# 160 small TensorE products without a reader, ahead of the first product and behind the last one

## The chip, the core and the metric

The kernel runs on one core of one Trainium2 chip. A core has five engines that work side by side, each with its own list of instructions in a fixed order: TensorE (PE, with its weight loads shown as PEld), VectorE (DVE), ScalarE (ACT), GpSimd (POOL) and SyncE (SP), which here only issues transfers. They wait for each other by semaphores. The metric is the time of one execution on the device in microseconds (us), and of a kernel the median of its runs.

## What is computed

The input is x of 16 batches with 512 tokens of 512 features in fp32. Each token is normalized and conditioned in six ways, by tables of gains and biases that two indices and a mask pick per token, and by three small networks on per-batch vectors. The six results are weighted, joined, and pass a two-layer network with silu and a last normalization; x is added. Cut to its core:

```python
h = _ln(x, pw_g[pathway_ids], pw_b[pathway_ids])
h = _ln(h, cp_g[compartment_ids], cp_b[compartment_ids])
t = _ln(x, tm_g[time_steps], tm_b[time_steps])
m = x + _mlp_ln(memory_state, ...)[:, None, :]       # and n, r alike
s = _ln(x, ms_g[scale_type], ms_b[scale_type])
w = jax.nn.softmax(aw)
cat = jnp.concatenate([w[0]*h, w[1]*t, w[2]*m, w[3]*n, w[4]*r, w[5]*s], axis=-1)
return x + _mlp_ln(cat, int_W1, int_b1, int_W2, int_b2, int_g, int_be)
```

`_ln` subtracts the mean, divides by the root of the variance plus 1e-5, and applies gain and bias. `_mlp_ln` is `silu(s @ W1 + b1) @ W2 + b2`, normalized.

## The kernel before

The 8192 tokens are sorted by their combination of two indices (15 groups, `NG`), so that a tile of 128 sorted tokens shares its tables nearly everywhere. The sorted tokens are worked on in 16 windows (`NW`) of four tiles each. For every window rows of x and of the tables are gathered by indirect DMA from POOL's queue, DVE and ACT normalize, DVE turns 32 by 32 blocks, SP's queue spreads the turned blocks over the partitions (L205), and TensorE multiplies: first layer in L404 and L452, second layer in L546, and for the last tiles L487. POOL scatters the finished rows to their places (L638). Which step stands behind which is written out by hand in three lists of names (ORDER, WINDOW, LAST); every engine works off its part of that order.

Ahead of the windows stands a start of some 70 us. The places of the tokens are counted there:

- POOL writes constants: `iota` tables, and `ident`, a 128 by 128 identity, written twice (`make_identity`, once among the constant tiles and once more in L727).
- DVE compares every token's group with all 15 groups (L798) and scans the result (L807).
- TensorE's first two products, L810 and L811, add up the counts of the partitions in front (`pc`); L815 and L816 add up the groups' beginnings (`pbg`).
- DVE adds `pc` to the scan (L829), masks it (L830) and reduces it to each token's place (L832).
- L845 is the first layer of the three small networks (`ph`). L896 multiplies one-hot tables, eight at a time, which DVE builds in L883 to L887; their sum `pn` is the sorted list of tokens, which everything behind it needs (the gathers of x among it).

At the end, the last window's second layer runs on TensorE in L487, tile by tile. Behind each tile come `last_add` (L607, DVE), the sum of squares (L612, ACT), root and inverse (L588, L596), `end_sum` (L603, DVE) and `put_out` (L638, POOL), which scatters 128 rows. The program ends when the last scatter has landed and the engines have met.

Results of TensorE lie in PSUM, in a pool of eight buffers (`ps`, all with the tag "p") that are handed out in turn: a new tile takes the buffer of the tile eight requests earlier and waits until that one is finished with. `psum(name)` asks for one buffer of 128 by 512. The names that the change touches are `psum`, `ident`, `L` (32, a quarter of the 128 partitions, `P`), and the places behind L809 and behind the last call of `run`.

Two products without a reader are already in the kernel: L1063 and L1069 multiply blocks of `wt` into a tile named `idle`.

Of the kernel before, what the change touches and what calls it, by code (L numbers as in the profile page):

```python
# [81 lines left out]
def kernel(ctx: ExitStack, tc: tile.TileContext, a: dict, out: bass.AP):  # L82
# [24 lines left out]
    nc = tc.nc  # L107
# [6 lines left out]
    L = P // Q  # L114
# [42 lines left out]
    ident = const.tile([P, P], F32, name="ident")  # L157
# [506 lines left out]
    def scratch(k, *shape):  # L664

        n = 1
        for m in shape:
            n *= m
        room, at = rooms[k]
        t = room[:, at : at + n]  # L670
        rooms[k][1] = at + n
        names = "abc"[: len(shape)]
        return t if len(shape) == 1 else t.rearrange(f"p ({' '.join(names)}) -> p {' '.join(names)}",
                                                     **dict(zip(names, shape)))
# [14 lines left out]
    for nm in ("mem", "noi", "res"):  # L689
        k = a[nm + "T"].shape[0]  # L690
        kk = min(k, P)
        n = k // kk
        t = prep.tile([kk, n, B], F32, name="stT" + nm)
        nc.scalar.dma_start(t, a[nm + "T"].rearrange("(c p) b -> p c b", p=kk))
        stT.append(t)
        t = w2[:kk, at : at + n, :]
# [16 lines left out]
    def iota(t, pattern, base=0, step=0):  # L713
        nc.gpsimd.iota(t, pattern, base=base, channel_multiplier=step, allow_small_or_imprecise_dtypes=True)
        return t

    i_row = iota(prep.tile([P, 1], F32, name="i_row"), [[0, 1]], step=1)
    i_col = iota(scratch(1, P), [[1, P]])
    i_grp = prep.tile([P, NG], F32, name="i_grp")
# [87 lines left out]
    nc.vector.tensor_tensor_scan(f_run, f_of, f_of, 0.0, ALU.add, ALU.max)  # L807
    upto = run[:, :, NQ - 1]
    pc = ps.tile([P, NG], F32, tag="p", name="pc")  # L809
    nc.tensor.matmul(pc, below, upto, start=True, stop=False)  # L810
    nc.tensor.matmul(pc[:, 1:], above, upto[:, : NG - 1], start=False, stop=True)  # L811
    nc.scalar.copy(up[:, 1:], upto)
# [639 lines left out]
    def piece(name):  # L1452
        kind, *at = name.split(".")
        if kind in pieces:
            pieces[kind](*map(int, at))
        elif kind in for_window:
            for_window[kind](of(at[0]))
        elif kind in for_tile:
            for_tile[kind](of(at[0]), *map(int, at[1:]))
        elif kind == "wu":  # L1460
            awake(at[0], [int(v) for v in at[1:-1]], int(at[-1]))
        elif kind == "tv":
            turn_v(of(at[0]), int(at[1]), home(at[0], "V"))
        elif kind[0] == "s":
            spread_row(of(at[0]), "r" + kind[1], "c" + kind[1], home(at[0], kind[1]), int(at[1]))
        else:
            layer1(of(at[0]), kind[1], int(at[1]))
# [6 lines left out]
    def run(names, w=None):  # L1474
        for name in names.split():
            kind, *at = name.split(".")
            if w is not None and at and at[0] in FROM:
                v = w + FROM[at[0]]
                if not 0 <= v < NW:
                    continue  # L1480
                name = ".".join([kind, str(v), *at[1:]])
            if name not in done:
                done.add(name)
                piece(name)
# [8 lines left out]
    for w in range(NW - 1):  # L1493
        run(WINDOW, w)
    run(LAST, NW - 1)


# [51 lines left out]
```

## Time and profile before

| what | value |
| --- | --- |
| median of 3 runs | 923.31 us |
| lowest and highest run | 919.57, 925.25 us |
| profiled execution, first to last instruction (its span) | 920.3 us |
| mean granted TensorE clock over the span | 0.994 |
| data moved over the span | 185.40 MB |

Nothing but its span is known of the profiled execution's own time; the span lies 3.0 us under the median and inside the range of the runs. In the profile, PE is TensorE, L followed by a number is a line of the kernel, and times are counted from the first instruction. A row names engine, line, operation, tiles (output, arrow, inputs), the shape on the array for TensorE (rows by columns of the weights), the shape of the moving data and its type. Times in order of time are start and length in us. Instructions of a kind that stand close together are merged into one row with their count; the length is then from the first start to the last end. An fp32 product is two pairs of a weight load and a product on the array, so four products in the code are eight rows on TensorE and eight weight loads.

### The profile page before, as it was taken

The numbers are of one execution on the slowest core, as the hardware profiler recorded it, in microseconds if no ns is written. First come the engines' busy times: TensorE is split into PE (matmuls) and PEld (weight loads), VectorE is DVE, ScalarE is ACT, GpSimd is POOL, SyncE is SP. The second block draws the span as 40 slices with busy tenths as digits, with TensorE's granted clock in tenths as the row PEclk, the third lists the DMA queues.
The fourth block names the chain that finished last, engine by engine and source line by source line (L and its number), as shares of the span: only waits on it lengthen the run. The fifth ranks groups of instructions, "written<-read, shape, count | busy, mean of one in ns | idle before, by whom it ended". The sixth has DMA issues, their size and how long they took to land.

```text
span 920.3 us, 13563 instructions
## 1 busy us (share of the span) xinstructions
PE 884.8 (96%) x3617; PEld 642.0 (70%) x3617; DVE 733.6 (80%) x1360; ACT 521.2 (57%) x1263; POOL 666.9 (72%) x730
## 2 busy tenths in 40 slices
PE   6979899999999999999999999999999999999996
PEld 6634446868677777868686877777686867778682
DVE  8776767878789798978787887869697888879565
ACT  5568736464555738374646556473657566572413
POOL 9876678576768678686878686877767676876452
PEclk9999999999999999999999999999999999999999
DMA  8755677777767777777777777777667776776513
GB/s 272 249 185 179 220 226 197 207 210 204 235 178 232 202 218 195 215 208 202 227 202 227 187 235 191 226 193 216 186 197 210 203 220 191 221 200 190 154 37 113
DMA packets 88557, 185.40 MB, mean 201 GB/s; under 512 B 24324, under 2 KB 24388, under 8 KB 88476
## 3 DMA queue, kind: packets, MB, share of 16 engines
q0 software_dynamic: 31104, 104.88, 39.4%
q1 hardware_dynamic: 56668, 79.53, 29.6%
q8 instruction: 30, 0.49, 0.2%
q14 instruction: 51, 0.42, 0.2%
q10 hardware_dynamic: 704, 0.08, 0.1%
HBM read 100.48 MB, written 19.97 MB: 131 GB/s over the span
## 4 chain that ended last, share of the span: by engine, by line
PE 50%; POOL 5%; DVE 4%; issue 3%; DMA 3%; SPq 2%; ACT 1%; POOLq 0%; DVEq 0%; ACTq 0%
PE u L452 13%; PE p L404 13%; PE p L452 11%; PE pq_0b L546 4%; PE pq_1b L546 4%; PE pq_1a L546 3%; PE pq_0a L546 2%; SPq L205 2%; DMA catZ<-rZ 2%; POOL xbs L391 1%; POOL out L638 1%; DMA pw<-in_pw,i_pw 1%; DVE vs L265 1%; DVE yb L634 0%; DVE yb L633 0%
## 5 line engine op out<-in xcount | busy, mean ns | idle before, releaser
L404 PE MATMUL p<-vs,catV 128*128 128x512 f32 x512 | 228.3, 593 | 3.9 <-DVE vs L265 1.7
L404 PEld LDWEIGHTS p<-vs,catV 128*128 128x128 f32 x512 | 96.9, 190 | 108.5 <-issue 99.6
L452 PE MATMUL p<-wh__81,catH 128*128 128x256 f32 x480 | 111.0, 379 | 0.0
L452 PEld LDWEIGHTS p<-wh__81,catH 128*128 128x128 f32 x480 | 91.4, 190 | 12.2
L376 ACT ACTIVATE pw<-pw,rsh 128x512 f32<-128x512 f32 x64 | 45.6, 714 | 95.2 <-DVE pw L383 76.9
L638 POOL DMA_INDIRECT out<-yb,tok x64 | 75.4, 1178 | 31.2 <-issue 15.1
L475 ACT ACTIVATE add<-add 128x512 f32<-128x512 f32 x64 | 39.7, 625 | 94.4 <-DVE add L472 93.1
L350 ACT ACTIVATE junk<-pw 128x512 bf16<-128x512 f32 x60 | 37.5, 626 | 85.8 <-DVE pw L347 78.1
L171 POOL DMA_INDIRECT cp<-cp_rows,i_cp x64 | 73.4, 1147 | 15.5 <-issue 13.2
L391 POOL TENSOR_TENSOR xbs<-xbs,rows 128x512 f32<-128x512 f32 x64 | 82.4, 1289 | 1.4
L171 POOL DMA_INDIRECT pw<-in_pw,i_pw x64 | 63.0, 984 | 28.1 <-DVE rH L197 13.0
L625 POOL TENSOR_TENSOR rsy<-vey,mhalf 128x4 f32<-128x4 f32 (+1 forms) x16 | 23.6, 1473 | 82.3 <-DVE veh L368 69.5
L171 POOL DMA_INDIRECT xbs<-in_x,tok x64 | 65.1, 1017 | 19.9 <-issue 18.1
L171 POOL DMA_INDIRECT add<-rows,i_add x64 | 67.0, 1048 | 16.6 <-issue 16.5
L383 DVE SCALAR_TENSOR_TENSOR pw<-pw,sumsh,cp 128x512 f32<-128x512 f32 x60 | 45.5, 760 | 32.9 <-DMA cp<-cp_rows,i_cp 32.8
L317 ACT ACTIVATE xm<-xbs,nmx,rsx 128x512 f32<-128x512 f32 x64 | 48.8, 806 | 22.9 <-DVE nmx L311 17.2
L372 POOL TENSOR_TENSOR rsh<-veh,mhalf 128x1 f32<-128x1 f32 x64 | 48.6, 760 | 13.0 <-DVE veh L368 11.5
L347 DVE SCALAR_TENSOR_TENSOR pw<-pw,rsx 128x512 f32<-128x512 f32 x64 | 56.0, 876 | 2.3
L452 PE MATMUL p<-wt,catH 128*128 128x256 f32 x240 | 56.7, 379 | 0.0
L452 PE MATMUL u<-wt,catX 128*128 128x256 f32 x240 | 56.5, 379 | 0.0
L452 PEld LDWEIGHTS u<-wx__80,catX 128*128 128x128 f32 x240 | 45.7, 190 | 12.6 <-issue 3.8
L452 PE MATMUL u<-wt,ss 128*128 128x256 f32 x240 | 54.4, 379 | 0.0
(439 smaller groups left out, 2127.7 us busy)
## 6 DMA issues: line engine op xcount, KB each, us to landing
catX<-rX SPq DMA_DIRECT2D x240, 64.0 KB
catV<-rV SPq DMA_DIRECT2D x240, 64.0 KB
catZ<-rZ SPq DMA_DIRECT2D x240, 64.0 KB
catH<-rH SPq DMA_DIRECT2D x240, 64.0 KB
rows<-adde SPq DMA_DIRECT2D x8, 256.0 KB
yb<-in_int_W SPq DMA_DIRECT2D x1, 1024.0 KB
catH<-in_int_W SPq DMA_DIRECT2D x1, 1024.0 KB
w1x<-in_int_W SPq DMA_DIRECT2D x1, 1024.0 KB
```

What stands on the lines that cost most here:

```text
L171: nc.gpsimd.indirect_dma_start(dst, None, table, bass.IndirectOffsetOnAxis(ap=idx, axis=0), **kw)
L317: nc.scalar.activation(t, st["xb"][:, j, :], AF.Identity, bias=st["nm"][:, j : j + 1], scale=st["rs"][:, j : j + 1])
L347: nc.vector.scalar_tensor_tensor(h, h, st["rs"][:, j : j + 1], pw[:, D:], ALU.mult, ALU.add)
L372: nc.gpsimd.tensor_tensor(rs, st.pop(("ve", j)), mhalf[:, :1], ALU.pow)
L376: nc.scalar.mul(pw[:, :D], pw[:, :D], st.pop(("rs", j)))
L383: nc.vector.scalar_tensor_tensor(pw[:, :D], pw[:, :D], st["sh", j][:, 1], cp, ALU.add, ALU.mult)
L391: nc.gpsimd.tensor_add(st["xb"][:, j, :], st["xb"][:, j, :], rows[:, 2, :])
L404: nc.tensor.matmul(st["p1", g], st["c" + blk][:, g, c, :], m[:, c, :], start=(blk == first and c == order[0]), stop=(blk == last and c == ...
L452: nc.tensor.matmul(dst, m[:, c], at_["half1"][k][:, c], start=(k == 1 and c == 0), stop=(c == NC - 1), skip_group_check=True)
L475: nc.scalar.activation(st["add", g], st["add", g], AF.Silu)
L546: nc.tensor.matmul(st["pq", 2 * p + i][:, half], st["zp", p][k][:, c], at_["half"][k][:, c], start=False, stop=(c == 1), skip_group_check= ...
L638: nc.gpsimd.indirect_dma_start(out_rows[j], bass.IndirectOffsetOnAxis(ap=tok[:, j, w : w + 1], axis=0), yb[:, j, :], None)
```

## The change

A helper asks for a PSUM tile and multiplies a 32 by 32 corner of `ident` with a 32 by 16 corner of it into the tile's first 32 partitions, `n` times into the same place. Nothing reads the result. It is called with 64 ahead of the first product, and with 96 behind the last step.

```diff
+    def idle_products(name, n):
+        t = psum(name)
+        for _ in range(n):
+            nc.tensor.matmul(t[:L, :L // 2], ident[:L, :L], ident[:L, : L // 2], start=True, stop=True)
...
     pc = ps.tile([P, NG], F32, tag="p", name="pc")
+    idle_products("idle0", 64)
     nc.tensor.matmul(pc, below, upto, start=True, stop=False)
...
     run(LAST, NW - 1)
+    idle_products("idle1", 96)
```

What stands on TensorE at the start, before. In brackets are the semaphores that a row waits for, named by the engine or the DMA queue that raises them. `pc`, `pbg` and `ph` are the tiles named above, `up` a column of counts, `room` scratch space, `w` a weight:

```order
L1545 UNCONDITIONAL_BRANCH [waits barrier_Pool_Activation_PE_DVE_SP_release]
L810 MATMUL pc<-vs_86,room_118 128x15 [waits DVE_49]
L811 MATMUL pc<-vs_86,room_118 128x14
L815 MATMUL pbg<-room_118,up 14x1 [waits Activation_49,Pool_49]
L815 MATMUL pbg<-room_118,up 14x1 x2
L816 MATMUL pbg<-up,room_118 128x14
```

And now:

```order
L1552 UNCONDITIONAL_BRANCH [waits barrier_Pool_Activation_PE_DVE_SP_release]
L720 MATMUL idle_232<-ident 32x16 [waits Pool_49]
L720 MATMUL idle_232<-ident 32x16 x63
L816 MATMUL pc<-vs_86,room_118 128x15 [waits DVE_49]
L817 MATMUL pc<-vs_86,room_118 128x14
L821 MATMUL pbg<-room_118,up 14x1 [waits Activation_49,Pool_49]
```

The 64 products wait for POOL once, for `ident`, and stand ahead of `pc` in TensorE's order; the lines behind are numbered 5 or 6 higher. On TensorE at the end, before (`p_15_1` and `p_15_3` are second-layer tiles of the last window, `catV` holds its turned input):

```order
L487 MATMUL p_15_1_8029<-w_82,catV 128x512 x3
L487 MATMUL p_15_3_8034<-w_82,catV 128x512 [waits DMAHW4_49,DMAHW5_49,DMAHW3_49,DMAHW2_49]
L487 MATMUL p_15_3_8034<-w_82,catV 128x512 x3
L1545 UNCONDITIONAL_BRANCH
```

And now:

```order
L487 MATMUL p_15_1_8094<-w_82,catV 128x512 x3
L487 MATMUL p_15_3_8099<-w_82,catV 128x512 [waits DMAHW4_49,DMAHW5_49,DMAHW3_49,DMAHW2_49]
L487 MATMUL p_15_3_8099<-w_82,catV 128x512 x3
L720 MATMUL idle_8136<-ident 32x16 [waits PE_49]
L720 MATMUL idle_8136<-ident 32x16 x95
```

The 96 products stand between the last product and the branch to the end; their first one waits for an earlier TensorE write into the same buffer. Of the instructions that were there before, one got a new wait: the first product of `ptp` (L1014, now L1020) waits for an earlier TensorE write. The other engines' instructions, their order and their waits are as before.

## Prediction

> **What bounds the kernel now.** I read the page first, then the order of time of the first 12 us and of the end, then windows for the clock, and last the TensorE rows whose shapes are near the added one.
>
> The page's first and second part, and the queue that brings instructions:
>
> ```profile
> span 920.3 us, 13563 instructions
> ...
> PE 884.8 (96%) x3617; PEld 642.0 (70%) x3617; DVE 733.6 (80%) x1360; ACT 521.2 (57%) x1263; POOL 666.9 (72%) x730
> ...
> PE   6979899999999999999999999999999999999996
> ...
> PEclk9999999999999999999999999999999999999999
> ...
> q8 instruction: 30, 0.49, 0.2%
> ```
>
> TensorE is busy in all but the first and the last slices, so a shift of the whole program costs its full length, and a delay inside the middle would too. The added work lies in the only two places where TensorE idles for long: ahead of its first product and behind its last. The question is how long these two holes are, and how long 64 and 96 products take in them.
>
> The first 12 us in order of time (start, length, engine, line, operation, and in brackets the idle time and who ended it):
>
> ```profile
> 2.59 0.29 POOL masks.py:199 TENSOR_SCALAR_AFFINE_SELECT ident<-ident 128x128 f32<-128x128 f32 x1
> ...
> 4.97 2.17 DVE L807 TENSOR_TENSOR_SCAN vs<-vs 128x960 f32<-128x960 f32 x1
> ...
> 7.20 0.61 PE L810 MATMUL pc<-vs,room 128*128 128x15 f32 x2 [7.20 <-DVE sm L818]
> ...
> 7.64 0.58 PE L811 MATMUL pc<-vs,room 128*128 128x14 f32 x2
> ...
> 8.27 1.16 DVE L829 TENSOR_TENSOR vs<-vs,pc 128x960 f32<-128x960 f32 x1 [0.49 <-PE pc L811]
> ...
> 9.15 0.32 PE L815 MATMUL pbg<-room,up 128*14 128x1 f32 x6 [0.92 <-POOL tokf L752]
> ...
> 9.46 1.16 DVE L830 TENSOR_TENSOR vs<-vs 128x960 f32<-128x960 f32 x1
> ```
>
> The added products read only ident, whose second writing on POOL ends at 2.59 + 0.29 = 2.88. TensorE's first product, L810, started at 7.20, when DVE's scan L807 was through. So the hole at the start runs from about 2.93 to 7.20, 4.27 us. Who waits behind it is in the same rows: DVE L829 stood idle for 0.49 us until pc was there. Whatever L810 is late, L829 is late.
>
> Windows (busy time of each engine with the number of instructions, then granted clock, DMA share, GB/s):
>
> ```profile
> core 0: us, PE busy (x) PEld busy (x) DVE busy (x) ACT busy (x) POOL busy (x), PEclk, DMA share, GB/s
> ...
> 9.46:31.26 21.80, 21.25 (x147) 20.42 (x146) 21.20 (x35) 15.68 (x47) 20.77 (x41) 1.00 1.04 377
> ...
> 39.50:42.90 3.40, 3.40 (x48) 2.02 (x49) 3.05 (x14) 0.00 (x0) 2.72 (x7) 0.50 0.71 198
> ...
> 56.60:59.90 3.30, 3.30 (x25) 0.92 (x17) 2.17 (x7) 3.30 (x7) 1.97 (x3) 0.50 0.09 24
> ...
> 911.50:916.70 5.20, 0.00 (x0) 0.00 (x0) 3.58 (x7) 1.02 (x3) 2.86 (x3) 1.00 0.26 101
> 916.80:918.50 1.70, 0.00 (x0) 0.00 (x0) 0.00 (x0) 0.00 (x0) 0.00 (x0) 0.50 0.40 154
> 918.50:920.30 1.80, 0.00 (x0) 0.00 (x0) 0.00 (x0) 0.00 (x0) 0.00 (x0) 0.50 0.00 0
> ```
>
> From L829's successor to the end of the one-hot tables DVE is busy 21.20 of 21.80 us: it has no slack to win back a late start. The end of the program, in order of time:
>
> ```profile
> 897.46 13.97 PE L487 MATMUL p<-w,catV 128*128 128x512 f32 x32
> ...
> 914.40 0.82 DVE L603 SCALAR_TENSOR_TENSOR yb<-yg,sd,xbs 128x512 f32<-128x512 f32 x1
> ...
> 915.76 0.96 POOL L638 DMA_INDIRECT out<-yb,tok  x1 [0.30 <-issue]
> ```
>
> The last product ends at 897.46 + 13.97 = 911.43; then come DVE, the last scatter on POOL to 916.72, its landing (a share of 0.40 up to 918.5, none behind it), and 1.8 us of closing steps without work. I let TensorE run until 918.0, in the middle of what is left of the landing, before anything waits for it: the second hole is 6.6 us.
>
> **The change, part by part.** 160 fp32 products make 640 instructions, so each is two weight loads and two products on the array; that is how the page counts its 3617 pairs. For 64 products that is 128 pairs, for 96 it is 192. What does a pair cost? The TensorE rows in order of time:
>
> ```profile
> 9.85 3.58 PE L845 MATMUL ph<-stTmem,w 128*128 128x16 f32 x16
> ...
> 15.56 5.39 PE L896 MATMUL pn<-vs 128*64 128x128 f32 x32 [0.32 <-DVE bi L917]
> ...
> 34.23 0.88 PE L1068 MATMUL pf<-ident,catZ 64*32 64x16 f32 x32
> ...
> 36.68 0.38 PE L1028 MATMUL pgc<-rows,catZ 14*128 14x64 f32 x2
> 36.91 0.38 PE L1029 MATMUL pgc<-rows,room 14*128 14x64 f32 x2
> 37.13 0.38 PE L1028 MATMUL pgc<-rows 14*128 14x64 f32 x2
> ...
> 39.31 1.23 PE L1058 MATMUL pa<-at_n,ident 128*32 128x16 f32 x32 [0.34 <-ACT at_n L1039]
> ```
>
> And two rows of the same load, 128 columns of fp32 weights, grouped by line and shape (the last number ahead of the second bar is the mean ns of one):
>
> ```profile
> L845 PEld LDWEIGHTS ph<-stTmem,w 128*128 128x128 f32 x16 | 3.5, 333 | 0.0
> ...
> L1063 PEld LDWEIGHTS idle<-wt 128*128 128x128 f32 x2 | 0.3, 188 | 0.0
> ```
>
> The load takes 333 ns at 10 us and 188 ns at 33 us. The start runs at a slow clock, although the clock's column stands at 1.00 there. Line L896 alone shows where it ends (its products in flight in each us):
>
> ```profile
> 18.00:19.00 1.00, 1.00 (x6) 1.00 1.05 387
> ...
> 20.00:21.00 1.00, 1.00 (x11) 1.00 1.06 389
> ```
>
> Up to 19 us six are in flight in a microsecond, afterwards eleven. So the first added products meet the slow clock, the last ones a fast one.
>
> The price of a pair at the slow clock: L845's 16 pairs take 3.58 us; less the 0.37 us of the last one that is 3.21 / 15 = 214 ns for weights of 128 columns and only 16 columns of data, so the load sets the pace. The added pair has 32 columns of weights: 214 / 4 = 53.5 ns. At the fast clock the four pairs from the first L1028 to the second take (37.13 - 36.68) / 4 = 112 ns each for 128 columns, so 28 ns for 32. From below both are bounded by rows with 32 columns of weights: L1068, (0.88 - 0.18) / 31 = 23 ns fast, and L1058, (1.23 - 0.21) / 31 = 33 ns in a stretch that is mostly slow (0.50 from 39.5). But these two write to the four quarters of the output in turn, while the added products all use the first 32 rows and the first quarter, one place on the array, as L845 and L1028 use the one whole array. So I take 53.5 slow and 28 fast, and keep 33 and 23 as lower ends.
>
> *Ahead of the first product.* 128 x 53.5 ns = 6.85 us from 2.93 to 9.78. L810 then starts 2.58 us late, L829 as well, and DVE carries it to 31.26. The sum: +2.58. L815, L816 and the ph products stand behind in TensorE's order; pbg had waited 0.92 us for POOL, so it is later by less, and ph has to be through before pn, which DVE's own delay puts at 15.56 + 2.58. Lower end: 128 x 33 = 4.2 us, through at 7.15, nothing late. Below nothing: the slow clock might end sooner; on DVE's path that could shorten only pc's own 1.0 us (8.27 - 7.20), by up to half, so -0.5.
>
> *Behind the last product.* 192 x 28 = 5.4 us, from 911.3 to 916.8, inside the hole of 6.6 us: nothing. What hides it is the last normalization and the scatter with its landing. If that cover is gone, or the clock is slow all the way, 192 x 53.5 = 10.3 us, 3.6 over the hole: +3.6 is the upper end. The clock fell to 0.50 just behind 916.7 here, 5.3 us after the last product, so a slow remainder would be a few products.
>
> *The rest.* The new tile ahead takes one of the eight PSUM buffers in turn; so ptp, the ninth tile instead of the eighth, waits for an earlier TensorE write that has long ended, and the tile behind takes a buffer that its reader left long before. Both cost under 0.1 us. Nothing is changed in the other queues. The 640 instructions need 2.5 more fetches (7234 instructions in 30 packets are 241 each); a fetch's time is 0.002 x 16 x 920 / 30 = 1.0 us of one engine, against 3.6 us in which 128 fast pairs use one up: hidden.
>
> Sum against the profiled execution: 920.3 + 2.6 = 922.9 for the span. The median of the runs, 923.31, stands 3.0 above that span; with the same distance I get 925.9.
>
> **A rule that would make it cheaper.** The row is L845's 214 ns for 128 columns at the slow clock, 112 in L1028. The Trainium skill, "TensorE: Matmul & The Clock Gate", section "LDWEIGHTS (loading the stationary operand)", gives the load as columns divided by 1.2, in ns, whatever the clock: 107 for 128 columns, 27 for 32. By that, an estimate, the first 128 pairs take 3.4 us, end at 6.4 and cost nothing. The fast rows agree with it, the slow ones do not, and the slow ones are at the place in question.
>
> **The rivals.**
>
> *Cheap products.* If the pace is that of L1058 and L1068, 23 to 33 ns, both holes swallow everything: 923.3. For it: the same size of weights. Against it: their four quarters.
>
> *The clock rises under the new products.* The windows show steps that last about 3.4 us (39.5 to 42.9, 56.6 to 59.9). If 3.4 us of unbroken products raise the clock, it is fast from somewhere between 6.3 and 9.8 us. At 8.0, 95 of the 128 pairs are through, the other 33 take 0.9 us: L810 at 8.9, 1.7 late, less some 0.4 in pc: 924.6. Against it: L845 and its successors ran unbroken from 9.85 to beyond 15 us and six a microsecond of L896 still stand at 18 to 19. The same page's section "The HAM clock gate (the "warmup" mystery)" has the rule of about 3.4 us of sustained activity; L845 disagrees if being occupied is enough for it.
>
> *The half-clock steps move.* The steps at 39.5 and 56.6 cost at most half of 3.4 us each; a start that is later by 2.6 us may lose them or win others, 3.4 us either way: 922.5 to 929.3.
>
> *Slower by over 1%.* The place is the first hole, and the mechanism is that products on one PSUM tile wait for each other: each then costs its full duration, 211 ns as in L1058: 128 x 0.211 - 4.27 = +22.7, and 192 x 0.18 - 6.6 = +28 behind the end, 974. With one price p for both, 320 p - 10.9 exceeds 9.2 us from 63 ns on. Against it: L845's products last 374 ns and start every 214, and the two halves of each of them write the same cells.
>
> **How the numbers follow.** Forecast 0.55 (925.9), cheap products 0.18 (923.3), the clock rises 0.10 (924.6), moved steps 0.07, a tail that sticks out 0.05 (929.5), over 1% slower 0.04, and 0.01 for a gain over 1% that none of these explains. About 1% (9.2 us) is what a measurement of this kernel can tell from no change, as its own runs lie 5.7 us apart. The bounds: -0.5 and -3.4 give 919.4, +2.6 and +3.6 give 929.5; I take 920.0 to 930.0, which also holds the runs' own spread around the middle cases. Faster by over 1% would need 9.2 us, more than all the gains named together: 0.01. Within 1%: 0.95. Slower: 0.04.
>
> **What would show it.** Right: the added products run from 2.9 to about 9.8 us at 53 ns, L810 starts 2.6 us later and L829 behind it, pn ends 2.6 us later; at the end the products run from 911.3 plus the shift for 5.4 us, and the closing steps keep their distance from the last scatter. Wrong: L810 at 7.2 as before (cheap), L845's load under 200 ns (clock risen), or a shift at 33 us that is gone by 100 us, since I assume that nothing between holds slack.

## The result, and the profile after

The changed kernel took 925.21 us in the median of 17 runs (921.69 to 928.67), the kernel before 919.85 in as many on the same chip (917.16 to 925.25). The ratio is 1.0051, interval 1.0034 to 1.0067, so the change costs 4.7 us (3.1 to 6.2): within 1%, but not nothing. (A difference in us is here and below the ratio less one, times the median before; the ratio is estimated from the single runs, and is not quite the quotient of the two medians.) The profiled execution took 928.67 us, the longest of the 17.

Its page, first and second part and the queue that brings instructions:

```profile
span 926.8 us, 14203 instructions
...
PE 902.8 (97%) x3937; PEld 658.4 (71%) x3937; DVE 729.8 (79%) x1360; ACT 520.7 (56%) x1263; POOL 667.3 (72%) x730
...
PE   8989999999999999999999999999999999989998
...
q8 instruction: 33, 0.54, 0.3%
```

TensorE has 320 pairs more (3937 against 3617), three fetches more on q8, and the span is 6.5 us longer. The first and the last slice of TensorE are fuller now, as they must be, and that is no gain: the products there are read by nobody.

The start in order of time, DVE's rows first and then TensorE's; L816 was L810 before, L835 was L829, L902 was L896:

```profile
4.97 2.17 DVE L812 TENSOR_TENSOR_SCAN vs<-vs 128x960 f32<-128x960 f32 x1
...
10.94 1.16 DVE L835 TENSOR_TENSOR vs<-vs,pc 128x960 f32<-128x960 f32 x1 [3.16 <-PE pc L817]
```

```profile
2.94 7.01 PE L720 MATMUL idle<-ident 32*32 32x16 f32 x128 [2.94 <-POOL ident masks.py:199]
9.87 0.61 PE L816 MATMUL pc<-vs,room 128*128 128x15 f32 x2
10.32 0.58 PE L817 MATMUL pc<-vs,room 128*128 128x14 f32 x2
...
18.37 6.09 PE L902 MATMUL pn<-vs 128*64 128x128 f32 x32 [1.46 <-DVE bi L923]
```

The scan L812 ends at 7.14 as before, and L816 could start; it starts at 9.87, behind the 128 pairs. DVE's L835 now stands idle for 3.16 us where L829 stood for 0.49: 2.67 more, the same as L816's delay (9.87 against 7.20). That is how a wait is read: the bracket names the tile and the line, and the difference of two such brackets is the price. At L902 it is 2.81 (18.37 against 15.56).

The end in order of time, and the windows over it:

```profile
916.43 7.31 PE L720 MATMUL idle<-ident 32*32 32x16 f32 x192
...
921.36 0.96 POOL L638 DMA_INDIRECT out<-yb,tok  x1 [0.30 <-issue]
```

```profile
916.50:920.90 4.40, 4.40 (x142) 4.40 (x142) 3.54 (x7) 1.02 (x3) 2.29 (x2) 1.00 0.18 63
921.10:923.70 2.60, 2.60 (x50) 2.54 (x48) 0.00 (x0) 0.00 (x0) 0.96 (x1) 0.50 0.54 203
```

Behind the last product the clock falls, 4.5 us later, while small products run: 142 pairs in 4.40 us, then about 50 in 2.60. They end at 923.74. The span ends 926.8 - 921.36 = 5.44 us behind the start of the last scatter; before it was 920.3 - 915.76 = 4.54. So 0.9 us of the loss sits behind that scatter, where I had put nothing. (Spans are given to 0.1 us, so such a distance is good to 0.05 us.)

Was it the products that were waited for, or the landing? The transfers in the 4.0 us from the start of the last scatter (each digit is 0.1 us, the mean busy share of the 16 DMA engines in tenths), the kernel before:

```profile
DMA  0078969972000009799796000000000000000000
...
DMA packets 160, 0.52 MB, mean 131 GB/s; under 512 B 32, under 2 KB 32, under 8 KB 160
```

And the changed kernel:

```profile
DMA  0078979972006009699694400010101000000000
...
DMA packets 161, 0.54 MB, mean 135 GB/s; under 512 B 32, under 2 KB 32, under 8 KB 160
...
q8 instruction: 1, 0.02, 1.5%
```

Each view holds two scatters: 128 rows of 512 fp32 numbers are 0.26 MB, half of the 0.52 MB. The burst up to 1.0 us belongs to the scatter before, whose POOL instruction ran just ahead, and the one from 1.5 us on to the last scatter. (A scatter that stands alone, at 911.66 in the kernel before, moves 80 packets, 0.26 MB, in one burst from 1.5 us on.) Before, it is all through at 2.2 us. In the changed kernel one packet of q8, a fetch of instructions of 0.54 MB / 33 = 16 KB, falls in at 1.2 us, and the last burst trails off up to 3.1 us with digits of 1: nearly all engines are done, a few small pieces are not. (That these are the pieces of the engine that carried the fetch is read from the digits; the view names no engines.) This is 0.9 us, the whole of the difference in distance. The products themselves had ended at 923.74, before 921.36 + 3.1 = 924.46.

That leaves 6.5 - 2.7 - 0.9 = 2.9 us of this execution. The path there was not a constant shift. L1069 (L1063 before), a product without a reader that was there already and stands behind `pn`, starts at 36.19 (33.38 before: +2.81) and the first window's ptH at 107.42 (104.99: +2.43), but near 795 us the shift was gone. The kernel before at these places, in order of time:

```profile
33.38 0.91 PE L1063 MATMUL idle<-wt 128*128 128x384 f32 x2
...
104.99 0.63 PE L1212 MATMUL ptH<-ident,pw 128*128 128x128 f32 x4 [0.86 <-ACTq L320]
...
795.18 7.03 PE L404 MATMUL p<-vs,catV 128*128 128x512 f32 x16
...
828.81 3.62 PE L452 MATMUL u<-wx__80,ss 128*128 128x256 f32 x16
832.26 3.62 PE L452 MATMUL u<-wt,ss 128*128 128x256 f32 x16
```

The changed kernel:

```profile
36.19 0.91 PE L1069 MATMUL idle<-wt 128*128 128x384 f32 x2
...
107.42 0.63 PE L1218 MATMUL ptH<-ident,pw 128*128 128x128 f32 x4 [0.86 <-ACTq L320]
...
794.51 7.03 PE L404 MATMUL p<-vs,catV 128*128 128x512 f32 x16
...
832.12 5.41 PE L452 MATMUL u<-wx__80,ss 128*128 128x256 f32 x16 [3.07 <-DVE ss L433]
837.36 3.62 PE L452 MATMUL u<-wt,ss 128*128 128x256 f32 x16
```

At 795 it is 0.7 us ahead; then TensorE waits 3.07 us for `ss`, and the next 16 products take 5.41 us instead of 3.62. From 0.7 ahead it goes to 837.36 - 832.26 = 5.10 behind. What held `ss` is a load of a window's input (line, awaited transfer, then total, times and longest in us over the whole execution; the longest is the wait here):

```profile
DVE ss L433 <- DMA catV<-rV: 6.9, 3, 5.1
```

Whether a late load there belongs to the change or to this execution is what the first thing to try, the same kernel once more, has to tell.

### The profile page after: what moved, and what is told of

It is laid out like the page before. It is cut to its first block, busy times and chain, and to the rows that moved or that the text cites. A ratio compares the mean times of both kernels' runs of the same rounds, so it can differ in the third digit from the quotient of the medians.

```text
span 926.8 us, 14203 instructions
## 1 busy us (share of the span) xinstructions
PE 902.8 (97%) x3937; PEld 658.4 (71%) x3937; DVE 729.8 (79%) x1360; ACT 520.7 (56%) x1263; POOL 667.3 (72%) x730
## 5 line engine op out<-in xcount | busy, mean ns | idle before, releaser
L452 PE MATMUL u<-wx__80,ss 128*128 128x256 f32 x240 | 56.2, 388 | 3.1 <-DVE ss L433 3.1
```

The source lines that it names most:

```text
L452: nc.tensor.matmul(dst, m[:, c], at_["half1"][k][:, c], start=(k == 1 and c == 0), stop=(c == NC - 1), skip_group_check=True)
```

## The experiments

The theory: the loss is the first hole (128 pairs of 53 ns end 2.7 us after the scan) plus a fetch in the last scatter; the tail's own products cost nothing. Rivals: the products behind the last one stick out; the clock is what the products change; the middle loses (the stall near 830). All kernels are edits of the changed kernel, and each ratio is to the kernel before in runs on the same chip.

| label | products ahead, behind | median (runs), before (runs) | ratio (interval) | in us |
| --- | --- | --- | --- | --- |
| front64 | 64, 0 | 925.46 (12), 923.64 (29) | 1.0021 (1.0001 to 1.0041) | +1.9 (0.1 to 3.8) |
| tail96 | 0, 96 | 921.49 (12), 923.64 (29) | 0.9987 (0.9967 to 1.0007) | -1.2 (-3.0 to 0.6) |
| front32 | 32, 0 | 922.22 (12), 923.64 (29) | 0.9996 (0.9974 to 1.0019) | -0.4 (-2.4 to 1.8) |
| tail192 | 0, 192 | 931.55 (6), 923.64 (29) | 1.0083 (1.0061 to 1.0105) | +7.7 (5.6 to 9.7) |
| again | 64, 96 | 925.40 (12), 921.35 (29) | 1.0036 (1.0014 to 1.0058) | +3.3 (1.3 to 5.3) |
| front128 | 128, 0 | 930.29 (6), 921.35 (29) | 1.0105 (1.0062 to 1.0148) | +9.7 (5.7 to 13.6) |
| wide16 | 16 full-width, 0 | 922.17 (12), 921.35 (29) | 1.0006 (0.9982 to 1.0030) | +0.6 (-1.7 to 2.8) |
| both_fit | 32, 64 | 920.85 (12), 921.35 (29) | 1.0000 (0.9976 to 1.0025) | 0.0 (-2.2 to 2.3) |
| fit64 | 64, 64 | 924.82 (12), 923.56 (17, one of 1899.38 us left out of the ratio) | 1.0032 (1.0000 to 1.0064) | +3.0 (0.0 to 5.9) |

**front64: the products ahead alone.**

```diff
-    idle_products("idle1", 96)
```

> Only the 64 products ahead of the first product; the 96 behind are gone. Theory (the start is late by what the products overrun their hole, 2.7 us, and that is carried to the end): pc starts at 9.87 instead of 7.20, pn ends 2.8 us later, and the time is 2 to 3 us over before. Rival A (the windows take the shift back, and the loss of the changed kernel comes from behind the end): pc is as late, but the time is within 1 us of before. Rival B (the later start moves the half-clock steps and costs more by that): 4 to 5 us over before with more half-clock time than before.

Measured: +1.9 us (0.1 to 3.8). The start costs something by itself, though the interval only just excludes nothing. Its span is 923.5, and the last scatter started at 918.97: 4.53 us to the end, as in the kernel before (4.54), and no fetch lies in it. So all of its 3.2 us of span lie ahead of that scatter.

**tail96: the products behind alone.**

```diff
-    idle_products("idle0", 64)
```

> Only the 96 products behind the last product. Theory (they end inside the landing of the last scatter): the same as before within 0.7 us, the closing steps at the same distance from the last scatter. Rival A: 2 to 3 us over before, with the landing of the last scatter or the meeting of the engines later by that. The products run at 28 to 31 ns a pair, and end about 6 us after the last product.

Measured: -1.2 us (-3.0 to 0.6), no loss that can be told from nothing. Its trace has a small one all the same. TensorE's rows, POOL's last scatter, and SP's wait behind them:

```profile
909.90 4.95 PE L720 MATMUL idle<-ident 32*32 32x16 f32 x142
...
915.11 0.45 PE L720 MATMUL idle<-ident 32*32 32x16 f32 x6 [0.26 <-issue]
...
915.85 2.48 PE L720 MATMUL idle<-ident 32*32 32x16 f32 x44 [0.29 <-issue]
```

```profile
914.30 0.96 POOL L638 DMA_INDIRECT out<-yb,tok  x1 [0.30 <-issue]
```

```profile
SPq L1551 <- PE idle L720: 0.9, 1, 0.9
```

Here the closing step waits 0.9 us for the products, which end at 918.33, 8.4 us after they began (about 6 were expected, and 7.31 stood in the changed kernel); the scatter is 919.4 - 914.30 = 5.10 us from the end, 0.6 more than before. So the second hole is full to the brim with 96 products, and in this execution they stick out a little. Two things make them longer here than in the changed kernel: the clock had fallen by 914.1, some 4 us after the last large product, and twice TensorE stood still for 0.26 and 0.29 us without a wait that the profile shows. What held it there is not shown.

This trace also has a fetch behind the last scatter, but a late one. The transfers in the 4.0 us from the scatter's start:

```profile
DMA  0069979992000009899797100070000000000000
```

The last burst is through at 2.3 us, although products run beside it all the time, and the fetch comes at 2.6, when it is over. So products beside the scatter did not lengthen its transfers.

**front32: half of the products ahead.**

```diff
-    idle_products("idle0", 64)
+    idle_products("idle0", 32)
...
-    idle_products("idle1", 96)
```

> Only 32 products ahead. 64 pairs at 53 ns are 3.4 us, from 2.94 to 6.35, inside the hole that ends at 7.20. Theory: pc starts at 7.2 as before, and the time is that of before within 0.7 us. If the mere presence of products, the new PSUM buffer or the wait of ptp cost something, pc is on time and the time is still 1 us or more over before.

Measured: -0.4 us, ratio 0.9974 to 1.0019. TensorE's first rows in order of time:

```profile
2.94 3.59 PE L720 MATMUL idle<-ident 32*32 32x16 f32 x64 [2.94 <-POOL ident masks.py:199]
7.20 0.61 PE L816 MATMUL pc<-vs,room 128*128 128x15 f32 x2 [0.67 <-DVE sm L824]
```

The products are through at 6.53, TensorE waits 0.67 us for DVE, and L816 starts at 7.20, as in the kernel before. So the hole does last until 7.20, and 3.59 us of products in it delay nothing.

**tail192: twice the products behind, alone.**

```diff
-    idle_products("idle0", 64)
...
-    idle_products("idle1", 96)
+    idle_products("idle1", 192)
```

> Only products behind the last one, but 192. 384 pairs take 10.8 us at 28 ns and up to 20 us at 53 ns, where the hole is 6.6 us. Theory: the end is late by what sticks out, 4 to 13 us depending on when the clock falls; about 8 us with the clock falling 4.5 us after the last product. If nothing waits for them, the same as before.

Measured: +7.7 us (5.6 to 9.7). The products' row, its windows, and SP's wait:

```profile
911.03 17.13 PE L720 MATMUL idle<-ident 32*32 32x16 f32 x384
```

```profile
911.10:916.40 5.30, 5.30 (x170) 5.30 (x170) 3.54 (x7) 1.02 (x3) 2.88 (x3) 1.00 0.18 67
916.60:928.00 11.40, 11.36 (x214) 11.25 (x211) 0.00 (x0) 0.00 (x0) 0.32 (x1) 0.50 0.10 35
```

```profile
SPq L1551 <- PE idle L720: 8.0, 1, 8.0
```

The closing step waits 8.0 us for TensorE and the time rises by 7.7; in the profile the end lies 929.2 - 915.96 = 13.24 us behind the start of the last scatter, 8.7 more than before. Its windows give both prices side by side: 170 pairs in 5.30 us are 31 ns each, 214 in 11.40 are 53 ns. The clock fell in the middle of unbroken products. A fetch falls into the last scatter here too, at 1.3 us after the scatter's start, and the transfers trail off as in the changed kernel, up to 3.2 us:

```profile
DMA  0069979972200509899695020001001100000000
```

**again: the changed kernel as it is.** No edit.

> The changed kernel as it is (64 ahead, 96 behind), beside the others on one chip. Theory (the late start costs about 2 us at the end, the products behind the end 0 to 1 us): 2 to 3.5 us over before. Rival (the two parts together cost more than apart): 4 to 6 us over, as in its first comparison.

Measured: +3.3 us (1.3 to 5.3) on another chip. The same stretch of the two profiled executions of the same code, 829 to 838 us, first that of the result:

```profile
829.00:838.00 9.00, 5.93 (x20) 4.90 (x20) 6.57 (x12) 0.60 (x2) 2.57 (x2) 0.81 0.48 118
```

Then again:

```profile
829.00:838.00 9.00, 9.00 (x44) 7.92 (x43) 8.21 (x15) 2.38 (x7) 5.33 (x5) 1.00 0.65 184
```

There TensorE is busy throughout at full clock and 20 pairs became 44. So the code does not bring the stall near 830 us by itself; it was seen in one execution of two, the longest of 17. What is the same in both is the end: the last scatter starts at 918.50 and the span ends at 924.0, 5.50 later, again with a fetch in it:

```profile
DMA  0069989974006009899697300010101000000000
...
q8 instruction: 1, 0.02, 1.5%
```

**front128: twice the products ahead, alone.**

```diff
-    idle_products("idle0", 64)
+    idle_products("idle0", 128)
...
-    idle_products("idle1", 96)
```

> 128 products ahead, none behind. 256 pairs at 53.3 ns are 13.6 us, so pc starts at 16.6 instead of 7.2, 9.4 us late. Theory (what the start loses comes through to the end, less what the waits of the middle take back): 7 to 9 us over before. Rival (the middle takes back a share of the loss, and not a fixed amount): 4 to 6 us. Rival (the clock rises under the products): pairs at 28 ns from some point on, and pc earlier than 14.

Measured: +9.7 us (5.7 to 13.6). TensorE's rows in order of time:

```profile
2.94 13.83 PE L720 MATMUL idle<-ident 32*32 32x16 f32 x256 [2.94 <-POOL ident masks.py:199]
16.70 0.61 PE L816 MATMUL pc<-vs,room 128*128 128x15 f32 x2
```

L816 starts 16.70 - 7.20 = 9.50 us late and the time is 9.7 higher, above the 7 to 9 that were expected, so a late start is carried through to the end, give or take the interval; in the single profile the last scatter starts 924.08 - 915.76 = 8.3 us later. The pairs take 13.76 / 256 = 54 ns over all of the 13.8 us, 34 of them still in the last 1.7 us: products of this size do not raise the clock in that time.

**wide16: sixteen full-width products in place of the 64 small ones.**

```diff
-            nc.tensor.matmul(t[:L, :L // 2], ident[:L, :L], ident[:L, : L // 2], start=True, stop=True)
+            nc.tensor.matmul(t[:, :P], ident, ident, start=True, stop=True)
...
-    idle_products("idle0", 64)
+    idle_products("idle0", 16)
...
-    idle_products("idle1", 96)
```

> Instead of the 64 small products 16 of the full width ahead (128 by 128 weights, 128 columns of data, each into a whole tile), none behind. 32 pairs at 213 ns are 6.8 us at the slow clock, as long as the 64 small ones. Theory (what raises the clock is how much of the array is used, and not how long it is occupied): the clock rises at a step between 6.3 and 9.8 us, the pairs after it take 107 ns, and pc starts between 8 and 9.8; load L845 takes under 200 ns if the clock holds. Since DVE sets the pace from pc to 31 us, the time is still 1 to 2.5 us over before. Rival: the clock stays slow until about 22 us as with the small products; pc at 9.9.

Measured: +0.6 us, ratio 0.9982 to 1.0030. TensorE's rows, the load of ph grouped by line and shape, and three windows:

```profile
2.94 5.66 PE L720 MATMUL idle<-ident 128*128 128x128 f32 x32 [2.94 <-POOL ident masks.py:199]
8.43 0.29 PE L816 MATMUL pc<-vs,room 128*128 128x15 f32 x2
```

```profile
L851 PEld LDWEIGHTS ph<-stTmem,w 128*128 128x128 f32 x16 | 1.9, 192 | 0.0
```

```profile
3.00:6.80 3.80, 3.80 (x18) 3.80 (x19) 3.73 (x8) 1.58 (x2) 3.56 (x6) 1.00 0.71 202
6.90:8.40 1.50, 1.50 (x16) 1.50 (x15) 0.81 (x5) 0.22 (x1) 1.10 (x6) 1.00 0.51 67
...
13.70:20.30 6.60, 3.97 (x19) 3.97 (x20) 6.39 (x15) 5.84 (x17) 6.51 (x12) 0.50 1.05 396
```

Full-width products do raise the clock. Up to 6.8 us 18 pairs take 3.80 us, 211 ns each, and then, from 6.9 on, 16 take 1.50, some 94 ns each. ph's load takes 192 ns here, in the changed kernel 333, as before:

```profile
L851 PEld LDWEIGHTS ph<-stTmem,w 128*128 128x128 f32 x16 | 3.5, 333 | 0.0
```

But it does not last. From 13.7 us the granted clock is 0.50, behind ph's products with 16 columns of data, and DVE is busy for 6.39 of those 6.60 us: it, and not TensorE, sets the pace. L816 starts 1.23 us late and is 0.32 shorter, so some 0.9 us of delay is left, and a faster clock at the start buys nothing that was measured. The time, +0.6, lies under the 1 to 2.5 that were expected, but its interval (-1.7 to 2.8) holds them all.

**both_fit: 32 ahead and 64 behind.**

```diff
-    idle_products("idle0", 64)
+    idle_products("idle0", 32)
...
-    idle_products("idle1", 96)
+    idle_products("idle1", 64)
```

> 32 products ahead and 64 behind, so that both end inside their holes: 3.4 us of 4.3 ahead, 3.6 us (6.8 at the slow clock) of 6.6 behind. Theory: the time is that of before within 0.7 us. If products cost something by being there, 1 us or more over.

Measured: 0.0 us, ratio 0.9976 to 1.0025. The same kind of products at both ends, in numbers that fit into the holes, cost nothing that 12 runs can tell (the interval is some 2 us to either side). Its span was 917.1 us, and the last scatter started at 912.62, 4.48 us from the end: the late fetch came ahead of that scatter, at 911.2.

**fit64: 64 ahead and 64 behind.** This keeps the late start and makes the tail short; it also has one fetch fewer than the changed kernel (32 against 33).

```diff
-    idle_products("idle1", 96)
+    idle_products("idle1", 64)
```

> 64 products ahead as in the change, 64 behind instead of 96. In both profiles of the changed kernel a fetch of 16 KB of TensorE's instructions falls into the last scatter, which then lands 3.7 us after its start instead of 2.7. With 64 behind the second of the two late fetches is not called for. Theory (the fetch delays the landing): the last scatter lands 2.7 us after its start, and the time is 2 to 3 us over before, about 1 us under the changed kernel. Rival (products that run beside the scatter slow it, or a later start does): 3.7 us as in the changed kernel.

Measured: +3.0 us (0.0 to 5.9). The products' row and POOL's last scatter:

```profile
912.62 4.38 PE L720 MATMUL idle<-ident 32*32 32x16 f32 x128
```

```profile
917.55 0.96 POOL L638 DMA_INDIRECT out<-yb,tok  x1 [0.30 <-issue]
```

The transfers in the 4.0 us from that start:

```profile
DMA  0078979972000009999896000000000000000000
...
DMA packets 160, 0.52 MB, mean 131 GB/s; under 512 B 32, under 2 KB 32, under 8 KB 160
```

No fetch in it, all through at 2.2 us, and the span ends 922.0 - 917.55 = 4.45 us behind the scatter, as before. The fetch came earlier, at 914.2, in the transfers of another scatter. These trail off in the same way, up to 3.1 us after that scatter's start at 912.92, but the end does not wait for them. With 64 products behind, TensorE is through before the last scatter starts, so this run alone does not tell the fetch from products beside the scatter; tail96 does.

With a fetch in the last burst the distance was 5.44 and 5.50; without one it was 4.54, 4.53 and 4.45 (before, front64, this one), and 4.49, 4.48, 4.53 and 4.52 in front32, both_fit, wide16 and front128. The times alone do not separate 3.0 here from 3.3 in again; the distances do, in one profile of each kernel.

## Why the prediction was right

**The first hole: right.** 53.5 ns for a pair was forecast, 6.93 / 128 = 54 ns measured from the first pair to L816; L816 later by 2.58 was forecast, by 2.67 measured. The wait went where the working put it, to L829 (now L835), and front32 and front128 bracket it: no delay with 64 pairs, 9.5 us with 256. The price was a quarter of that of 128 columns, with the reason that all products use one place on the array, while L1058 and L1068 use four. The price came true at the slow clock; no run changes the place, so the reason is not shown.

**The carry to the end: right within the intervals, weaker than put in one execution.** I assumed that nothing between holds slack. front128's 9.7 us (5.7 to 13.6) for 9.50 and front64's 1.9 (0.1 to 3.8) for 2.67 agree with it; neither excludes that a part is taken back. And a single pair of profiles shows +2.81, +2.43 and then -0.67 us at 795, where the same code stands at 796.16 in again, +0.98: executions of one kernel differ (921.69 to 928.67 us over its 17 runs) by more than this whole effect, and a shift of 2.7 us can't be followed through one trace to its end.

**The tail's own products: right in the end, mis-sized in the price.** I took 28 ns for a pair at the fast clock, from loads of 128 columns divided by four; the changed kernel's 142 pairs in 4.40 us and tail192's 170 in 5.30 are 31 ns each. The clock also fell 4.5 us behind the last large product although TensorE was occupied, and 50 pairs took the slow price, so 96 products took 7.31 us instead of 5.4. The hole was given 6.6 us and the landing had moved back; they stayed covered. In tail96, where they took 8.4 us, 0.9 us of them was waited for.

**The fetches: the step that was mis-sized.** "Hidden" was put at nothing, by comparing the 1.0 us that a fetch takes of one DMA engine with the 3.6 us in which TensorE uses one up. (640 instructions at 241 each are 2.7 fetches, not 2.5; three were measured.) That answers whether TensorE starves; in the changed kernel its 192 pairs run without a gap. It does not answer what else waits for that DMA engine. In the changed kernel a fetch falls into the last scatter, and the landing that ends the program comes 0.9 us later, so the sign that the closing steps keep their distance from the last scatter failed. Three last scatters with a fetch in their burst (the changed kernel, again, tail192) trail off to 3.1 or 3.2 us, and the eight others are through by 2.3, tail96's with products running beside it among them. The Trainium skill, "Runtime: NRT & Kernel Launch", section "Instruction fetch mechanics", calls crossing a 16 KiB block "mostly hidden": no run here shows a cost in time of the other fetches, but the one that meets the last transfer is not hidden.

**The sum.** 2.67 + 0.9 = 3.6 us lies in again's interval (1.3 to 5.3) and in that of the first comparison (3.1 to 6.2); the forecast's 2.6 lies only in the first of these two. That 925.9 came out so near 925.21 is partly luck: 923.31, from which I counted, is 3.5 us above the 919.85 that 17 runs gave, and the distance of 3.0 us from span to time that I took from it is 1.9 in the profiled execution (928.67 - 926.8). The increase is what the prediction should be judged by, and it was 0.7 us (again) to 2.1 us (the first comparison) short. About 1 us between 3.6 and the first comparison's 4.7 is not explained, and within its interval.

**The rivals.** Cheap products: no; a pair takes 54 ns at the start, and 31 ns, inside that rival's 23 to 33, only at the fast clock. The clock rises under the new products: no, front128 excludes it for products of this size over 13.8 us, wide16 shows that it does for large ones. Products that wait for each other on one PSUM tile: no, a pair takes 54 ns and not 211. A tail that sticks out: seen in tail96 and tail192, not in the changed kernel. Moved half-clock steps: one near 832 us, in one execution of two. The start has more of them too (mean granted clock of the first 100 us 0.97 before, 0.93 in the changed kernel, 0.95 in again), but tail96, which has no late start, also stands at 0.95. So no run ties them to the change; what makes a load of a window late near 830 us stays open.

## What to carry to other kernels

An idle stretch on an engine has a length, and what is put into it is free up to that length and costs one for one beyond it, as far as these intervals tell: read its start and end from the neighbours' waits, and price the filler by a row with the same clock. Instructions cost fetches too: behind the end of the work, ask not only whether the engine starves, but which transfer a fetch would delay. A shift of a few microseconds is judged from medians and from the distance between neighbouring events, not from the length of two single traces.

## What the hardware showed that I had not expected

Being occupied is not what raises or holds the clock. 13.8 us of unbroken 32 x 32 products left a pair at 54 ns, whereas sixteen products of 128 x 128 by 128 had the load at 192 ns instead of 333 by 10 us. At the other end the clock went to 0.50 some 4.5 us (the changed kernel) or 5.4 us (tail192) behind the last large product, with TensorE busy all the time; in both_fit it was only 2.7 us (it reads 1.00 up to 910.3 and 0.50 from 910.5, and the last large product ended at 907.75). In the Trainium skill, "TensorE: Matmul & The Clock Gate", the section 'The HAM clock gate (the "warmup" mystery)' speaks of about 3.4 us of sustained activity; wide16 agrees with that in order of size (L720 began at 2.94 and its pairs were fast from 6.9 on), front128 only if small products don't count as activity.

One fetch of 16 KB, 6% of the 0.26 MB that the last scatter moves, put off the end of its transfers from 2.2 to 3.1 us after the scatter's start.
